# A two-layer kernel on one core: the state update ahead of the gate product, new windows for the planner, keys scaled on ScalarE, and a masked block made one slot earlier

## The chip, the core and the metric

The kernel runs on one core of a Trainium2 chip. A core has five engines with queues of their own: TensorE (PE, matmuls into PSUM), VectorE (DVE), ScalarE (ACT), GpSimd (POOL, which works on SBUF only here) and SyncE (SP, which issues the DMAs). An engine works through its own queue in order, and waits on semaphores for the others. The metric is the device time of one execution in microseconds (us); lower is better.

## The reference, cut to what matters

Two transformer-like layers over 2 x 1024 tokens of width 256. The first layer adds to the residual a gated delta-rule attention with 32 value heads (16 key heads, 128 wide) and a routed low-rank FFN; the second adds a gated linear attention and an FFN with 2:4 sparsity. The change is in the delta-rule attention only:

```
qkvz = x @ W_qkvz                      # q, k, v, z per head
q, k, v = silu(causal_conv(q, k, v))   # depthwise, 4 taps
beta = sigmoid(b); g = -exp(A_log) * softplus(a + dt_bias)
q, k = l2norm(q) / sqrt(128), l2norm(k)
for each token t:                      # per head, S is 128 x 128
    S     = S * exp(g[t])
    delta = (v[t] - k[t] @ S) * beta[t]
    S     = S + outer(k[t], delta)
    o[t]  = q[t] @ S
y = rmsnorm(o * silu(z)) * norm_w @ W_out
```

## The kernel before, in words

**Tiling.** The recurrence is done in chunks of 64 tokens of both batch rows at once: the two rows fill the lower and the upper 64 partitions. A head group is 4 value heads with 2 key heads; there are 8 groups. A unit is 512 columns (4 chunks) of one group, a pair is two chunks of a unit, so there are 64 pairs, 8 to a group. Inside a chunk the tokens' mutual dependence is a triangular matrix per head, which is inverted by blocks: blocks of 8 on VectorE (`pair_lanes`), then joined to 16, 32 and 64 by small matmuls on TensorE (`pair_inverse`).

**The chain of a chunk** (`chunk_state`). TensorE multiplies the state S with keys and queries (pks and pqs, L729). VectorE subtracts pks from the values (vtok, L732) while ScalarE scales pqs (qs, L737). TensorE applies the inverse (pf, L742), GpSimd decays S (L745), ScalarE evacuates pf (f, L750), and TensorE forms the state's increment pS (L757) and the output's inner part po (L761). Then VectorE adds po to qs (L765), multiplies with the gate z (L767), and adds pS to S (L774). The next chunk's pks needs that S.

**Around the chain.** `chunk_tokens` transposes keys and values of a chunk to token order: keys go through PSUM (pk, L689), a ScalarE copy to SBUF (kt, L692) and a GpSimd product with a weight per head and token (ktok, L697); values through pv (L701) and ScalarE (vtok, L706). `chunk_norm` squares and sums on ScalarE (gsq, L784) and makes the norm on GpSimd (L789 to L796). `chunk_output` transposes on TensorE (yT, L806), evacuates on ScalarE (yTs, L809), multiplies with W_out (out, L813) and adds to the residual on VectorE (res, L816). `conv_block` projects (pj, L152), evacuates twice on ScalarE (raw L356, conv L358) and applies three taps on VectorE (L364); the SiLU (L373) is done by ScalarE at the next block. `pair_scores` makes decays and scores: a scan on VectorE (L510), an exponential on ScalarE (L512, with a table load), products on GpSimd (L514) and VectorE (np, L520), and DMAs by SP that lay the scores out again (nat L524, natd L530, n L534). `pair_lanes` ends with E (L586) on VectorE and two DMAs through DRAM (ed L588, U L590). `pair_inverse` begins with a masked copy of the scores on GpSimd (natm, L629) and a transpose of U on VectorE (L635), then px and pyt (L607) twice, with a second masked copy between.

**The order is planned.** Each engine's order of instructions is the order in which the program emits them. A slot p emits work for several pairs at once: projections and scores of pair p, the inverse of pair p-1, the states of pair p-2, the outputs of pair p-3. Each of these is a generator with a window (lo, hi) in the slot, and `in_windows` always advances the one whose next step is due first, where step n of a chain of m steps is due at lo + (hi - lo) * (n + 0.5) / m. So a window decides where in every engine's queue an instruction stands. Odd slots also hold a unit's norms (`unit_squares`, `unit_sums`, `unit_norms`).

Of the kernel before, what the change touches and what calls it, by code (L numbers as in the profile page):

```python
# [9 lines left out]
F32 = mybir.dt.float32  # L10
AF = mybir.ActivationFunctionType
ALU = mybir.AluOpType
AX = mybir.AxisListType

P = 128
# [10 lines left out]
HPG = 4  # L26
KPG = 2
# [6 lines left out]
B = 32  # L34
# [21 lines left out]
def bcast(ap, axis, n):  # L56
    a = ap.unsqueeze(axis)
    shape = list(a.shape)
    shape[axis] = n
    return a.to_broadcast(shape)  # L60
# [218 lines left out]
PH = PC * HPG  # L279
# [269 lines left out]
def pair_lanes(k, pools, pr):  # L549


    nc, n = k.nc, pr.n8
    X = k.X8[pr.index % 2]
    new = lambda tag, *shape: pools.work.tile([P, *shape], F32, tag=tag, name=f"{tag}{pr.name}", bufs=1)
    flat = lambda a: a.rearrange("p r c -> p (r c)")
    op = nc.vector.tensor_tensor

    def at(a, r, c, *dims):

        return bass.AP(a.tensor, flat(a)[:, r * W + c : r * W + c + 1].offset, [list(flat(a).ap[0])] + [[i * W + j, m] for i, j, m in dims])  # L560

    nc.vector.tensor_copy(at(X, 0, 1, (2, 2, 4)), at(n, 0, 1, (2, 2, 4)))

    two, row, col = (4, 4, 2), (1, 0, 2), (0, 1, 2)
    still = (0, 0, 2)
    t = new("t8", W, W)
    t4 = at(t, 0, 0, (1, 0, 2), (0, 1, 2))
    op(t4, at(n, 0, 2, two, row), at(X, 2, 3, two, still), ALU.mult)
    nc.vector.tensor_copy(at(X, 0, 2, two, row), at(n, 0, 2, two, row))
    yield  # L570
    op(at(X, 0, 3, two, row), at(n, 0, 3, two, row), t4, ALU.add)
    op(t4, at(X, 1, 2, two, col), at(X, 0, 1, two, still), ALU.mult)
    yield
    op(at(X, 0, 2, two, col), at(X, 0, 2, two, col), t4, ALU.add)

    t64 = new("t64", 4, 4, 4)
    T = new("T8", 4, 4)
    four = lambda i, j: (i, j, 4)
    op(t64, at(n, 0, 4, four(1, 0), four(0, 0), four(0, 1)), at(X, 4, 4, four(0, 0), four(0, 1), four(1, 0)), ALU.mult)
    yield  # L580
    nc.vector.tensor_reduce(T, t64, AX.X, ALU.add)
    op(t64, at(X, 0, 0, four(1, 0), four(0, 0), four(0, 1)), bcast(T.rearrange("p k c -> p c k"), 1, 4), ALU.mult)
    yield
    nc.vector.tensor_reduce(at(X, 0, 4, four(1, 0), four(0, 1)), t64, AX.X, ALU.add)
    E = pools.work.tile([P, W, B // W, W], F32, tag="E", name=f"E{pr.name}", bufs=1)
    op(E, bcast(X, 2, B // W), bcast(bcast(k.place, 1, W), 3, W), ALU.mult)  # L586
    ed = k.dram.tile([P, W, B], F32, tag="ed", name=f"ed{pr.name}", bufs=2)
    nc.sync.dma_start(ed, E.rearrange("p r q c -> p r (q c)"))  # L588
    pr.U = pools.work.tile([P, PH, B], F32, tag="U", name=f"U{pr.name}")
    nc.sync.dma_start(pr.U, bass.AP(ed.tensor, ed.offset, [[B, P], [P * B, PH], [1, B]]))  # L590
    yield


def pair_decays(k, pools, pr):
# [19 lines left out]
def pair_inverse(k, pools, pr):  # L614

    nc, wk = k.nc, pools.work
    flat = lambda a: a.rearrange("p a c -> p (a c)")
    new = lambda tag, s, n=B, **kw: wk.tile([P, PH, n], F32, tag=tag, name=f"{tag}{s}_{pr.name}", **kw)
    nat = pr.nat.rearrange("p x h c -> p (x h) c")

    def masked(s):

        out = new("natm", s)
        nc.gpsimd.tensor_tensor(out, nat, bcast(k.lowT[:, s - 3, :], 1, PH), ALU.mult)  # L629
        return out  # L630

    U = pr.U
    join = masked(3)
    L = new("L", 3)
    nc.vector.transpose(flat(L), flat(U))  # L635
    yield
    for s in (3, 4):
        px = part(k, f"px{s}_{pr.name}", B)
        blocks32(k, px, join, L)
        if s < 4:  # L640
            join = masked(s + 1)
        yield
        xs = new("xs", s)
        nc.scalar.copy(xs, px)
        yield
        pyt = part(k, f"pyt{s}_{pr.name}", B)
        blocks32(k, pyt, xs, U)
        yield
        nc.vector.tensor_tensor(U, U, pyt, ALU.add)  # L649
        L = new("L", s + 1)  # L650
        nc.vector.transpose(flat(L), flat(U))
        if s < 4:
            yield


    pr.invT = k.invT[pr.index % len(k.invT)]
    invT = pr.invT.rearrange("p x h c -> p (x h) c")
    full = pr.np[:, 0].rearrange("p x h c -> p (x h) c")
    for n, r in enumerate(QUARTERS):
        (nc.gpsimd.tensor_copy, nc.scalar.copy)[n % 2](invT[r, :, r], U[r])  # L660
    yield
    px = part(k, f"px5_{pr.name}", B)
    for i in range(PH):
        for q in (0, 2):
            lo, hi = QUARTERS[q], QUARTERS[q + 1]
            nc.tensor.matmul(px[hi, i, :], full[lo, i, B:CT], L[lo, i, :], start=True, stop=True)
    yield
    xs = new("xs", 5)
    for q, copy in ((1, nc.scalar.copy), (3, nc.vector.tensor_copy)):
        copy(xs[QUARTERS[q]], px[QUARTERS[q]])  # L670
    yield
    pyt = part(k, f"pyt5_{pr.name}", B)
    for i in range(PH):
        for q in (0, 2):
            lo, hi = QUARTERS[q], QUARTERS[q + 1]
            nc.tensor.matmul(pyt[lo, i, :], xs[hi, i, :], U[hi, i, :], start=True, stop=True)
    yield
    for q, copy in ((0, nc.scalar.copy), (2, nc.vector.tensor_copy)):
        copy(invT[QUARTERS[q], :, QUARTERS[q + 1]], pyt[QUARTERS[q]])
    yield  # L680


def chunk_tokens(k, pools, x):

    nc, wk, h, c = k.nc, pools.work, x.h, x.c
    if not x.last:
        pk = four(k, f"pk{x.name}")
        for m in range(KPG):
            nc.tensor.transpose(pk[:, m, :], of_chunk(h.kq[m][:, 0], c), k.ident)  # L689
        yield  # L690
        kt = wk.tile([P, KPG, P], F32, tag="kt", name=f"kt{x.name}", bufs=1)
        nc.scalar.copy(kt, pk[:, 0:KPG, :])  # L692
        yield
        x.k = wk.tile([P, HPG, P], F32, tag="ktok", name=f"ktok{x.name}")
        pair = lambda a: a.rearrange("p (m i) c -> p m i c", m=KPG)
        wend = h.wend[:, c, :].rearrange("p (m i) -> p m i", m=KPG)
        nc.gpsimd.tensor_tensor(pair(x.k), bcast(kt, 2, 2), bcast(wend, 3, P), ALU.mult)  # L697
        yield
    pv = four(k, f"pv{x.name}")
    for i in range(HPG):  # L700
        nc.tensor.transpose(pv[:, i, :], of_chunk(h.v[i], c), k.ident)  # L701
    yield
    x.v = wk.tile([P, HPG, P], F32, tag="vtok", name=f"vtok{x.name}")
    for m in range(KPG):
        two = slice(2 * m, 2 * m + 2)
        nc.scalar.activation(x.v[:, two, :], pv[:, two, :], AF.Copy, scale=h.norm[:, c, m : m + 1])  # L706
        yield


def chunk_state(k, pools, x, scored=None):  # L710
# [3 lines left out]
    nc, wk, h, c = k.nc, pools.work, x.h, x.c  # L714
# [7 lines left out]
    if not x.first:  # L722
        pks, pqs = four(k, f"pks{x.name}"), four(k, f"pqs{x.name}")
        for s, out in ((0, pks), (1, pqs)):
            for m in range(KPG):
                two = slice(2 * m, 2 * m + 2)
# [8 lines left out]
        qs = wk.tile([P, HPG, P], F32, tag="qs", name=f"qs{x.name}")  # L735
# [13 lines left out]
    f = wk.tile([P, HPG, P], F32, tag="f", name=f"f{x.name}")  # L749
# [8 lines left out]
    po = four(k, f"po{x.name}")  # L758
# [1 line left out]
        for b, rows in halves:  # L760
            nc.tensor.matmul(po[rows, i, :], x.pair.np[rows, 1, x.at, i, :], f[rows, i, :], start=True, stop=True)  # L761
    yield
    no = po
    if not x.first:
        nc.vector.tensor_tensor(qs, qs, po, ALU.add)  # L765
        no = qs
    nc.vector.tensor_tensor(x.z, no, x.z, ALU.mult)  # L767
    yield
    if not x.last:
        for b in range(NB):  # L770
            if x.first:
                nc.scalar.copy(k.S[:, b], pS[b])
            else:
                nc.vector.tensor_tensor(k.S[:, b], k.S[:, b], pS[b], ALU.add)  # L774
    yield


# [79 lines left out]
def delta_layer(k, I):  # L857
    nc, tc = k.nc, k.tc
    with ExitStack() as ctx:
        pool = lambda name, bufs: ctx.enter_context(tc.tile_pool(name=name, bufs=bufs))  # L860
        pools = Pools()
# [32 lines left out]
        for p in range(NPAIR):  # L894
            pr = Pair()
            u, n = divmod(p, UCHUNK // PC)
            pr.index, pr.h, pr.name, pr.chunks = p, k.units[u], f"{k.units[u].name}_{n}", []
            for i in range(PC):
                x = Chunk()
# [6 lines left out]
        pair = lambda p: k.pairs[p] if 0 <= p < NPAIR else None  # L906
# [3 lines left out]
        with tc.manual_schedule(engines=ordered):  # L910
            for p in range(-2, NPAIR + 3):
# [24 lines left out]
                if pair(p - 2):  # L936
                    one, two = pair(p - 2).chunks
                    add("tokens1", 0.0, 0.4, chunk_tokens(k, pools, two))
                    add("state0", 0.0, 0.5, chunk_state(k, pools, one, pair(p)))
                    add("state1", 0.5, 1.0, chunk_state(k, pools, two), "state0", "tokens1")  # L940
                    add("norm0", 0.5, 0.95, chunk_norm(k, pools, one), "state0")
                if pair(p - 3):
                    one, two = pair(p - 3).chunks
                    add("output0", 0.0, 0.25, chunk_output(k, pools, one))
                    add("norm1", 0.0, 0.5, chunk_norm(k, pools, two))
                    add("output1", 0.55, 0.85, chunk_output(k, pools, two), "norm1")
                in_windows(k, *work)
                if pair(p) and pair(p + 2):
                    pair_decays(k, pools, pair(p + 2))
# [539 lines left out]
```

## Time and profile before

| | us |
|---|---|
| median of three runs (2954.29 to 2967.72) | 2966.99 |
| the profiled execution's own time | 2959.04 |
| its span | 2957.3 |
| until the delta layer is in steady work (FFN, gates) | about 300 |
| delta layer, 69 slots | about 2350 |
| second layer | about 307 |

In the delta layer's 2350 us (300 to 2650) PE is busy for 2119.1, VectorE 1723.5, ScalarE 1516.9, GpSimd 1441.5; the mean granted clock of TensorE is 0.97. A busy row is an average over the stretch: what sets the time is read from the waits of the engine that leads, and from the order of the instructions within one slot. In the timeline a row gives start and duration in us, engine, source line, operation, output and inputs with their shapes, the count of merged instructions, and in brackets the idle time before it with what ended it.

### The profile page before, as it was taken

How to read it: one execution, taken by the hardware profiler on the slowest of the kernel's cores; microseconds unless marked ns; L12 is line 12 of the kernel's file. 1: busy time of each engine (PE TensorE's matmuls, PEld its weight loads, DVE VectorE, ACT ScalarE, POOL GpSimd, SP SyncE). 2: the span in 40 equal slices, each digit the busy share in tenths (PEclk: the TensorE clock that was granted, in tenths of full speed). 3: DMA queues.
4: the chain of work that ended last, by engine and by line, in shares of the span. 5: the costliest groups of instructions: out<-in, count | busy, mean ns of one | idle time of the engine just before them, and what ended most of it. 6: DMA issues, size and time to landing. Idle time of an engine off the chain costs nothing.

```text
span 2957.3 us, 87624 instructions
## 1 busy us (share of the span) xinstructions
PE 2644.5 (89%) x36502; PEld 1703.3 (58%) x36502; DVE 2035.0 (69%) x3845; ACT 1723.9 (58%) x4121; POOL 1500.3 (51%) x2690
## 2 busy tenths in 40 slices
PE   6997599989989998999899989998999899889997
PEld 2444356656666666666666666666566666654465
DVE  7652577677876777777778777777787777645544
ACT  4432566666666666666666666666666676544321
POOL 2220366656665666666656665666666656630000
PEclk9998799999999999999999999999999999989999
DMA  2001111111111111111111111111111111110000
GB/s 76 4 1 57 28 31 37 31 37 38 35 35 39 35 35 35 42 28 42 28 45 28 42 34 36 28 42 35 36 32 36 28 32 26 23 56 3 1 15 15
DMA packets 265965, 95.21 MB, mean 32 GB/s; under 512 B 220513, under 2 KB 244193, under 8 KB 265569
## 3 DMA queue, kind: packets, MB, share of 16 engines
q1 hardware_dynamic: 261872, 86.67, 13.0%
q8 instruction: 287, 4.70, 0.7%
q10 hardware_dynamic: 3696, 2.95, 0.3%
q14 instruction: 110, 0.89, 0.1%
HBM read 53.63 MB, written 27.53 MB: 27 GB/s over the span
## 4 chain that ended last, share of the span: by engine, by line
PE 54%; DVE 15%; ACT 13%; POOL 10%; issue 4%; SPq 3%; DMA 2%; DVEq 0%; ACTq 0%; POOLq 0%
DVE conv L364 6%; PE pj L152 5%; PE pks L729 5%; PE z L152 5%; PE out L813 5%; PE pqs L729 4%; POOL rn L445 3%; PE pf L742 2%; PE yT L806 2%; PE y L1107 2%; PE pg L152 2%; PE base L152 2%; PE pd L1339 2%; ACT L512 2%; DVE z L767 2%
## 5 line engine op out<-in xcount | busy, mean ns | idle before, releaser
L364 DVE SCALAR_TENSOR_TENSOR conv<-raw,convw,conv 128x512 f32<-128x512 f32 x768 | 719.1, 936 | 177.1 <-ACT conv L358 153.8
L152 PE MATMUL pj<-xnT,w 128*128 128x512 f32 x1024 | 501.7, 614 | 8.6 <-DMA w<-in_W_qkvz 8.6
L729 PE MATMUL pks<-S,kq 128*64 128x256 f32 x960 | 176.5, 414 | 130.4 <-DVE S L774 90.3
L152 PEld LDWEIGHTS pj<-xnT,w 128*128 128x128 f32 x1024 | 181.3, 192 | 173.2 <-issue 168.2
L745 POOL TENSOR_TENSOR S<-S,eEnd 128x512 f32<-128x512 f32 x224 | 263.3, 1195 | 25.7 <-PE pqs L729 11.7
L813 PE MATMUL out<-wo,yTs 128*128 128x256 f32 x1024 | 252.3, 390 | 3.1 <-ACT yTs L809 3.1
L152 PE MATMUL z<-wz,xnT 128*128 128x512 f32 x512 | 248.0, 607 | 0.0
L361 POOL COPY tails<-raw 128x6 f32<-128x6 f32 x192 | 47.0, 245 | 362.3 <-ACT raw L356 361.4
L813 PEld LDWEIGHTS out<-wo,yTs 128*128 128x128 f32 x1024 | 190.7, 192 | 55.6 <-issue 28.6
L660 POOL COPY invT<-U 32x256 f32<-32x256 f32 x128 | 49.7, 388 | 317.5 <-DVE U L649 313.8
L729 PEld LDWEIGHTS pks<-S,kq 128*64 128x64 f32 x960 | 80.8, 142 | 221.4 <-issue 110.1
L356 ACT COPY raw<-pj 128x512 f32<-128x512 f32 x256 | 146.4, 572 | 103.4 <-PE pj L152 65.4
L737 ACT ACTIVATE qs<-pqs,neG 128x128 f32<-128x128 f32 x480 | 136.0, 365 | 119.0 <-PE pqs L729 119.0
L784 ACT ACTIVATE gsq<-z 128x128 f32<-128x128 f32 x512 | 159.0, 311 | 61.7 <-DVE z L767 52.5
L358 ACT ACTIVATE conv<-pj,convw 128x512 f32<-128x512 f32 x256 | 176.8, 691 | 0.0
L697 POOL TENSOR_TENSOR ktok<-kt,wend 128x512 f32<-128x512 f32 x120 | 138.6, 1155 | 70.4 <-ACT kt L692 69.8
L729 PE MATMUL pqs<-S,kq 128*64 128x256 f32 x960 | 173.7, 415 | 0.0
L732 DVE SCALAR_TENSOR_TENSOR vtok<-pks,neG,vtok 128x128 f32<-128x128 f32 x480 | 134.1, 342 | 45.5 <-PE pks L729 45.5
L373 ACT ACTIVATE kq<-conv 128x512 f32<-128x512 f32 x128 | 80.6, 630 | 141.8 <-DVE conv L364 141.1
L742 PEld LDWEIGHTS pf<-vtok,invT 128*128 128x128 f32 x1024 | 131.9, 193 | 46.1 <-issue 17.3
L607 PE MATMUL px<-L,natm 32*32 32x32 f32 x8192 | 99.0, 194 | 54.0 <-DVE L L635 24.2
L774 DVE TENSOR_TENSOR S<-S,pS 128x512 f32<-128x512 f32 x224 | 143.5, 682 | 0.8
(323 smaller groups left out, 6080.4 us busy)
## 6 DMA issues: line engine op xcount, KB each, us to landing
lb<-grows SPq DMA_DIRECT2D x128, 128.0 KB
natd<-np SPq DMA_DIRECT2D x128, 128.0 KB
w<-in_W_qkvz SPq DMA_DIRECT2D x16, 512.0 KB
nat<-np SPq DMA_DIRECT2D x256, 32.0 KB
n<-natd SPq DMA_DIRECT2D x512, 4.0 KB
ed<-E SPq DMA_DIRECT2D x64, 128.0 KB
U<-ed SPq DMA_DIRECT2D x64, 128.0 KB
wz<-in_W_qkvz SPq DMA_DIRECT2D x16, 256.0 KB
```

Of the source, the lines that this page charges most:

```text
L152: k.nc.tensor.matmul(ps, lhsT_of(kt), rhs_of(kt), start=(kt == 0), stop=(kt == KT - 1))
L356: nc.scalar.copy(chunks(raw[:, :, KSIZE - 1 :]), pv)
L358: nc.scalar.activation(chunks(y), pv, AF.Copy, scale=tap(KSIZE - 1))
L364: nc.vector.scalar_tensor_tensor(y, shifted, tap(j), y, ALU.mult, ALU.add)
L697: nc.gpsimd.tensor_tensor(pair(x.k), bcast(kt, 2, 2), bcast(wend, 3, P), ALU.mult)
L729: nc.tensor.matmul(out[rows, two, :], q, k.S[:, b, two, :], start=True, stop=True)
L737: nc.scalar.activation(qs[:, i, :], pqs[:, i, :], AF.Copy, scale=at(k.neG, i))
L742: nc.tensor.matmul(pf[:, i, :], invT[:, i, :], x.v[:, i, :], start=True, stop=True)
L745: nc.gpsimd.tensor_tensor(k.S[:, b], k.S[:, b], bcast(k.eEnd[:, b, t, h.h0 : h.h0 + HPG], 2, P), ALU.mult)
L774: nc.vector.tensor_tensor(k.S[:, b], k.S[:, b], pS[b], ALU.add)
L784: nc.scalar.activation(sq, x.z[:, i, :], AF.Square, accum_out=x.sumsq[:, i : i + 1])
L813: nc.tensor.matmul(po[:, 0:D], yT[:, i, :], wo[:, i, :], start=(i == 0), stop=(i == HPG - 1))
```

## The change

Five edits, all in the delta layer:

1. In `chunk_state` the two additions to S stand ahead of qs and z, as a step of their own.
2. Windows: the two states' chains end at 0.46 and 0.96 of the slot instead of 0.5 and 1.0; norm0 lies from 0.47 to 0.9 (0.5 to 0.95); output0 from 0.08 to 0.33 (0 to 0.25); output1 from 0.6 to 0.85 (0.55 to 0.85).
3. In `chunk_tokens` the copy kt and the GpSimd product are replaced by four ScalarE activations that read the transposed keys from PSUM and write ktok with the weight as their scale.
4. The masked copy becomes a function `joining`; the first one of a pair is made in the last step of `pair_lanes`, a slot earlier than the inverse that uses it.
5. The second masked copy uses the same function at its old place.

```diff
@@ pair_lanes
     nc.sync.dma_start(ed, E.rearrange("p r q c -> p r (q c)"))
+    pr.join = joining(k, pools, pr, 3)
     pr.U = pools.work.tile([P, PH, B], F32, tag="U", name=f"U{pr.name}")
...
+def joining(k, pools, pr, s):
+
+    out = pools.work.tile([P, PH, B], F32, tag="natm", name=f"natm{s}_{pr.name}")
+    nat = pr.nat.rearrange("p x h c -> p (x h) c")
+    k.nc.gpsimd.tensor_tensor(out, nat, bcast(k.lowT[:, s - 3, :], 1, PH), ALU.mult)
+    return out
@@ pair_inverse
-    U = pr.U
-    join = masked(3)
+    U, join = pr.U, pr.join
...
-            join = masked(s + 1)
+            join = joining(k, pools, pr, s + 1)
@@ chunk_tokens
-        kt = wk.tile([P, KPG, P], F32, tag="kt", name=f"kt{x.name}", bufs=1)
-        nc.scalar.copy(kt, pk[:, 0:KPG, :])
-        yield
         x.k = wk.tile([P, HPG, P], F32, tag="ktok", name=f"ktok{x.name}")
-        pair = lambda a: a.rearrange("p (m i) c -> p m i c", m=KPG)
-        wend = h.wend[:, c, :].rearrange("p (m i) -> p m i", m=KPG)
-        nc.gpsimd.tensor_tensor(pair(x.k), bcast(kt, 2, 2), bcast(wend, 3, P), ALU.mult)
-        yield
+        for i in range(HPG):
+            nc.scalar.activation(x.k[:, i, :], pk[:, i // 2, :], AF.Copy, scale=h.wend[:, c, i : i + 1])
+            if i % 2:
+                yield
@@ chunk_state
-    no = po
-    if not x.first:
-        nc.vector.tensor_tensor(qs, qs, po, ALU.add)
-        no = qs
-    nc.vector.tensor_tensor(x.z, no, x.z, ALU.mult)
-    yield
     if not x.last:
         for b in range(NB):
             if x.first:
                 nc.scalar.copy(k.S[:, b], pS[b])
             else:
                 nc.vector.tensor_tensor(k.S[:, b], k.S[:, b], pS[b], ALU.add)
+        yield
+    no = po
+    if not x.first:
+        nc.vector.tensor_tensor(qs, qs, po, ALU.add)
+        no = qs
+    nc.vector.tensor_tensor(x.z, no, x.z, ALU.mult)
     yield
@@ delta_layer
-                    add("state0", 0.0, 0.5, chunk_state(k, pools, one, pair(p)))
-                    add("state1", 0.5, 1.0, chunk_state(k, pools, two), "state0", "tokens1")
-                    add("norm0", 0.5, 0.95, chunk_norm(k, pools, one), "state0")
+                    add("state0", 0.0, 0.46, chunk_state(k, pools, one, pair(p)))
+                    add("state1", 0.5, 0.96, chunk_state(k, pools, two), "state0", "tokens1")
+                    add("norm0", 0.47, 0.9, chunk_norm(k, pools, one), "state0")
...
-                    add("output0", 0.0, 0.25, chunk_output(k, pools, one))
+                    add("output0", 0.08, 0.33, chunk_output(k, pools, one))
...
-                    add("output1", 0.55, 0.85, chunk_output(k, pools, two), "norm1")
+                    add("output1", 0.6, 0.85, chunk_output(k, pools, two), "norm1")
```

## The prediction, made before the changed kernel was run

> **What bounds the kernel now.** I read the page first: its engine row and its clock row.
>
> ```profile
> PE 2644.5 (89%) x36502; PEld 1703.3 (58%) x36502; DVE 2035.0 (69%) x3845; ACT 1723.9 (58%) x4121; POOL 1500.3 (51%) x2690
> PEclk9998799999999999999999999999999999989999
> ```
>
> PE leads and no engine is full. The linear-attention layer runs from about 0.3 to 2.65 ms, in slots of one chunk pair each. So I asked second who PE waits for, from 600 to 2400 us (columns: sum, times, longest):
>
> ```profile
> PE pks L729 <- DVE S L774: 68.2, 31, 3.1
> PE pks L729 <- ACT kq L373: 27.5, 12, 2.6
> PE yT L806 <- POOL z L796: 26.3, 25, 1.8
> PE px L607 <- POOL natm L629: 9.6, 6, 1.6
> ```
>
> All PE waits there sum to 150 us of 1800. The period of eight slots (one head group) is 290.3 us (the same wait, at 918.78 and at 1209.07), 36.3 a slot, so 3.0 us of a slot is waiting. Third, I read one even slot, 1004.9 to 1040.35, by engine. PE:
>
> ```profile
> 1020.65 1.98 PE L152 MATMUL pj<-xnT,w 128*128 128x512 f32 x4
> 1024.67 1.37 PE L729 MATMUL pks<-S,kq 128*64 128x256 f32 x7 [2.04 <-ACT kq L373]
> ```
>
> VectorE before that moment:
>
> ```profile
> 1019.37 1.31 DVE L364 SCALAR_TENSOR_TENSOR conv<-raw,convw,conv 128x512 f32<-128x512 f32 x1 [0.81 <-ACT conv L358]
> 1020.61 0.67 DVE L765 TENSOR_TENSOR qs<-qs,po 128x512 f32<-128x512 f32 x1
> 1021.31 0.69 DVE L767 TENSOR_TENSOR z<-qs,z 128x512 f32<-128x512 f32 x1
> 1021.92 0.74 DVE L364 SCALAR_TENSOR_TENSOR conv<-raw,convw,conv 128x512 f32<-128x512 f32 x1
> 1022.59 0.68 DVE L520 TENSOR_TENSOR np<-lb,kq 128x512 f32<-128x512 f32 x1
> 1023.18 0.74 DVE L364 SCALAR_TENSOR_TENSOR conv<-raw,convw,conv 128x512 f32<-128x512 f32 x1
> 1023.85 1.28 DVE L774 TENSOR_TENSOR S<-S,pS 128x512 f32<-128x512 f32 x2
> ```
>
> The first S ends near 1024.5 and pks starts at 1024.67: the wait is for S even where the row names kq. S stands behind five instructions that the next chunk's pks does not need. This happens mid-slot in six or seven slots of eight, for 2.0 to 3.1 us. The second chunk's S, at the slot's end, costs 0.4 to 0.8 at most.
>
> **S ahead of qs and z.** By the due times S of the first chunk is now due at 0.361 of the slot, z at 0.427; the order becomes conv, S, conv, np, qs, z, conv. S comes earlier by 1023.85 - 1020.61 = 3.2 us, more than the wait. Taken alone, the mid-slot wait falls to nothing. What is late next follows from the other edits.
>
> **The output's window, 0 to 0.25 becoming 0.08 to 0.33.** This is the term that costs. Before, yT is due at 0.031 and its evacuation yTs at 0.094, ahead of qs (0.107). Now pks and pqs go first, yT is due at 0.111, yTs at 0.174, and the matmul group out at 0.236 instead of 0.156. ACT's order becomes qs, two ktok, gsq, the exponential of lb (0.135), two ktok (0.167), yTs, xs, f. PE's order is pqs, pk, yT, px, pf, pv, out. ACT's rows in this slot:
>
> ```profile
> 1011.35 1.14 ACT L737 ACTIVATE qs<-pqs,neG 128x128 f32<-128x128 f32 x4 [2.15 <-PE pqs L729]
> 1012.36 0.32 ACT L784 ACTIVATE gsq<-z 128x128 f32<-128x128 f32 x1
> ...
> 1013.23 1.28 ACT L512 ACT_TABLE_LOAD   x1
> 1014.52 0.63 ACT L512 ACTIVATE lb<-lb 128x512 f32<-128x512 f32 x1
> 1015.06 0.35 ACT L644 COPY xs<-px 128x256 f32<-128x256 f32 x1
> ```
>
> From start to next start, counted from the end of pqs (1011.21): 0.14 to qs, qs 1.01, ktok pair 0.51, gsq pair 0.87, table load and exp 1.83, ktok pair 0.51, yTs 0.49 (1008.34 to 1008.83), about 0.1 to PE: 5.46 us. PE has meanwhile pk 0.31, yT 0.49, px 0.68, pf 0.89, pv 0.44 = 2.81. So **out waits 2.65 us** where nothing waited before; everything behind it on PE (pj, pyt, pS, po, px, pj, pks) moves with it. The trace has no such wait. Its ends: 0, if ACT ran ahead, which is excluded as qs itself waits for pqs; and 3.75, if no two activations overlap (qs and ktok 4 x 0.365 each, gsq 2 x 0.503, exp 1.28 + 0.63, yTs 0.58, 0.14 and 0.1). I take 2.65, since starts in the trace follow one another that way.
>
> [...]
>
> **The slot, summed** (even, us from its first pj; PE steps from this slot's starts). pj 1.72, kq 0.93, pks 0.86, pqs 0.97 end at 4.5. Out starts at 9.95; out 1.83, pj 1.81, pyt 0.68, pS 0.93, po 0.98, px 0.69, pj 1.8 bring pks to 18.7; before, it stood at 1024.67 - 1004.91 = 19.76. Is S there? ACT, after yTs at 9.85: xs, f, vtok 1.22, table and kq 1.83, then raw and conv behind pj (13.6) until 14.8; DVE conv 15.5, S 16.8. Yes, by 1.9. But qs, z and two convs, once done before pks, now follow S: z ends near 19.5, the last conv at 20.1. gsq of that z (ACT) stands ahead of the next raw and conv, ending 22.1; conv and vtok reach 23.9. pf of the second chunk, ready at 23.8, waits 0.2; L for px5 comes at 25.4, another 0.5. From px5 to the end as before, 9.06. Sum 34.55 against 35.44: **0.9 gained** in an even slot. An odd slot has 0.6 more on ACT (silu and square of the keys) before vtok, and ssr now follows pf: pf waits 0.8; gain about 0.35. This includes the POOL wait of yT (0.6 to 0.9), which disappears because yT stands behind pks.
>
> **Keys scaled by ACT.** Per chunk a copy (46.1/120 = 0.38 us of ACT) and a POOL product (1.155) go; four activations from PSUM come. The same form is the qs row (PSUM, 128x128, per-row scale): 0.25 to 0.365 each, taken as 136.0/480 = 0.28. ACT +0.75 per chunk, +90 us in all, already counted above where it lies in front of yTs (1.02 of the 2.65); for the other chunk ACT has room ahead of out (yTs near 26, out after 27). POOL loses 139 us of cover that nobody waited for; DVE, whose conv stretches from 0.71 to 1.6 us, may gain: 0 to 20 us, taken as 0.
>
> **First masked block with the lanes.** One POOL instruction, 0.73 us, moves from the slot's start to the previous slot's end, behind z. Its input landed half a slot earlier. Behind it stand small norm steps and the tails copy, which POOL's idle time covers; uncovered it would cost 0.7. It ends the px wait of 1.6 us once a group.
>
> **S ahead of the lanes' last step.** S of the second chunk now precedes E, so E's two DMAs leave 1.3 us later. U landed 4.0 us after E where L waited for it (1224.62 to 1228.64). L then starts about 3.4 us into the slot, vtok at 5.0 to 6.1, pf is ready at 6.0: 0.1 late, inside out's wait. With S gone early, pks at the slot's start waits for nothing. The shorter chain windows do nothing else to the order.
>
> **Sum.** A group has three regular even slots, two regular odd ones, and three around its start and end that I count at zero: 3 x 0.9 + 2 x 0.35 + 1.6 = 5.0 us; eight groups 40; in the drain four chunks save qs and z, 5. Profiled execution 2959.0 - 45 = 2914; the median of the runs, 2967, stands 8 above that execution: **2922**.
>
> **The clock.** After the mid-slot waits PE often runs at half clock: granted 0.61 and 0.54 from 1316 to 1320, after a wait of 2.03. A mean of 0.98 to 0.99 is 30 to 45 us over the layer. [...]
>
> **Rivals.**
> - More than that: out's wait doesn't trip the clock, or POOL's relief speeds DVE. For it: out is preceded by dense work. Against: equal length. 2922 - 45 = **2877**. Chance 0.17.
> - A trade one for one: out's wait equals the wait removed, and pf, px5 take the rest. **2967**, within 0.5%, which is what a measurement here can tell from no change. Chance 0.13.
> - Slower: ACT ahead of yTs. If its chain takes 6.55 rather than 5.46, each of the eight slots loses 1.1 more: 8 x 8 x 1.1 = 70 against 45 gained, **2992**. It decides from 0.7 us per slot, a chain of 6.2. For it: the single durations in the page; against: the starts in the timeline. Chance 0.20.
> - The change as summed, 2890 to 2950: chance 0.50.
>
> Eight of ten: 2865 to 2990. Faster by over 0.5%: 0.67; within: 0.13; slower: 0.20.
>
> **What would show it.** Right: pks <- S nearly gone from PE's waits, out <- yTs new at 2 to 3 us in most slots, yT <- z gone, px <- natm gone, ACT near 1815 us, POOL near 1360. Wrong: no wait at out (then ACT does run ahead, and the gain is over 100 us), out waiting over 3.3 us, or L waiting for U past 6 us of the slot.

## The result, and the profile after

| | before | after |
|---|---|---|
| median, us (four runs each) | 2963.3 | 3044.2 |
| lowest to highest | 2954.3 to 2967.7 | 3028.0 to 3054.9 |
| ratio to before, 95% interval | 1 | 1.027 [1.022, 1.033] |
| profiled execution / span | 2959.0 / 2957.3 | 3054.9 / 3053.1 |
| PE busy / not busy within the span | 2644.5 / 312.8 | 2707.1 / 346.0 |

The change costs 81 us. Of the 95.8 us between the two spans, only 33.2 are waiting: 62.6 are TensorE being busy longer with the same 36502 instructions. The page after, engine row and clock row:

```profile
PE 2707.1 (89%) x36502; PEld 1721.4 (56%) x36502; DVE 2012.4 (66%) x3845; ACT 1798.9 (59%) x4481; POOL 1337.1 (44%) x2570
PEclk9998899999999999999999999999999999999999
```

The clock row is cut to tenths and hides it; the mean granted clock from 600 to 2400 us fell from 0.99 to 0.96, over the whole span from 0.971 to 0.955. In both traces the granted clock is 1.00 or 0.50. Time at half clock rose from 175 us to 278 in the whole span (from 51 to 150 between 600 and 2400). In the kernel after, the matmuls of a pj follow one another at 0.85 us at half clock and at 0.43 at full, those of out at 0.43 and 0.22. If half of the time at half clock is lost, an estimate from these steps, the clock accounts for at most 51 of the 62.6 us. What PE waits for from 600 to 2400 us (sum, times, longest):

```profile
PE out L810 <- ACT yTs L806: 100.6, 44, 2.9
PE pf L739 <- DVE vtok L729: 25.6, 32, 1.7
PE px L666 <- DVE X L562: 12.9, 14, 1.1
```

The old waits (pks for S, yT for z, px for natm) are gone. One wait stands in their place, out for yTs, about as long and as frequent as the old one of pks. PE around it, in the even slot from 1028.45:

```profile
1035.49 0.60 PE L698 MATMUL pv<-ident,v 128*128 128x128 f32 x4
1038.99 2.67 PE L810 MATMUL out<-wo,yTs 128*128 128x256 f32 x8 [2.89 <-ACT yTs L806]
1041.45 2.94 PE L152 MATMUL pj<-xnT,w 128*128 128x512 f32 x4
```

Out and pj normally take 1.99 and 1.88 us. Here they take 5.61 together instead of 3.87, 1.7 us more; the granted clock from 1040.16 to 1043.58 is 0.50. Between 600 and 2400 us out has 41 waits of more than 0.3 us; behind 32 of them the matmul groups of the next 8 us take at least 0.5 us more than usual (a group's lower quartile in the same kernel), 66 us in all. ScalarE in the same slot:

```profile
1031.31 0.31 ACT L781 ACTIVATE gsq<-z 128x128 f32<-128x128 f32 x1 [2.00 <-DVE z L771]
...
1032.57 0.57 ACT L356 COPY raw<-pj 128x512 f32<-128x512 f32 x1
1033.04 0.69 ACT L358 ACTIVATE conv<-pj,convw 128x512 f32<-128x512 f32 x1
1033.62 1.14 ACT L734 ACTIVATE qs<-pqs,neG 128x128 f32<-128x128 f32 x4
...
1036.02 1.28 ACT L512 ACT_TABLE_LOAD   x1
1037.32 0.63 ACT L512 ACTIVATE lb<-lb 128x512 f32<-128x512 f32 x1
1037.85 0.61 ACT L693 ACTIVATE ktok<-pk,wend 128x128 f32<-128x128 f32 x2
1038.35 0.58 ACT L806 COPY yTs<-yT 128x512 f32<-128x512 f32 x1
```

From the end of pqs (1033.01) to out (1038.99) are 5.98 us, not the 5.46 of the sum. The difference stands at the top: the first squares gsq of the second chunk's z wait 2.00 us for z, which now comes behind S, E and two convs. raw and conv follow them in ScalarE's queue, so qs starts 0.61 late; in the next slot it is 1.06 (pqs ends 1070.23, qs starts 1071.29). The sum had let ScalarE wait for pqs. Over the stretch:

```profile
ACT gsq L781 <- DVE z L771: 203.8, 83, 3.3
```

### The profile page after: what moved, and what is told of

Read it like the earlier page. It is cut to its first block, busy times and chain, and to the rows that moved or that the text cites. A ratio compares the mean times of both kernels' runs of the same rounds, so it can differ in the third digit from the quotient of the medians.

```text
span 3053.1 us, 88002 instructions
## 1 busy us (share of the span) xinstructions
PE 2707.1 (89%) x36502; PEld 1721.4 (56%) x36502; DVE 2012.4 (66%) x3845; ACT 1798.9 (59%) x4481; POOL 1337.1 (44%) x2570
## 4 chain that ended last, share of the span: by engine, by line
ACT 32%; PE 31%; DVE 27%; issue 4%; DMA 3%; POOL 2%; SPq 2%; ACTq 0%; DVEq 0%; POOLq 0%
DVE conv L364 9%; PE out L810 6%; PE pj L152 6%; ACT gsq L781 4%; DVE S L765 4%; ACT conv L358 4%; ACT raw L356 3%; ACT ktok L693 3%; ACT qs L734 3%; ACT L512 2%; DVE z L771 2%; DVE qs L769 2%; ACT sq L420 2%; PE y L1104 2%; ACT yTs L806 2%
## 5 line engine op out<-in xcount | busy, mean ns | idle before, releaser
L364 DVE SCALAR_TENSOR_TENSOR conv<-raw,convw,conv 128x512 f32<-128x512 f32 x768 | 671.8, 875 | 196.1 <-ACT conv L358 168.4
L810 PE MATMUL out<-wo,yTs 128*128 128x256 f32 x1024 | 305.1, 450 | 135.6 <-ACT yTs L806 135.3
L813 DVE TENSOR_TENSOR res<-res,out 128x256 f32<-128x256 f32 x128 | 53.9, 421 | 240.0 <-PE out L810 238.1
L739 PE MATMUL pf<-vtok,invT 128*128 128x128 f32 x1024 | 153.1, 293 | 35.3 <-DVE vtok L729 33.6
L786 POOL TENSOR_TENSOR ms<-sumsq,q 128x4 f32<-128x4 f32 x128 | 44.3, 346 | 271.6 <-ACT gsq L781 271.4
L693 ACT ACTIVATE ktok<-pk,wend 128x128 f32<-128x128 f32 x480 | 151.9, 376 | 1.6
L445 POOL TENSOR_TENSOR rms<-ms,mhalf 128x4 f32<-128x4 f32 x128 | 141.1, 1103 | 1.7
L754 PE MATMUL pS<-f,ktok 64*64 64x128 f32 x3840 | 132.5, 275 | 9.4 <-ACT f L747 9.4
L793 POOL TENSOR_TENSOR z<-z,rms 128x512 f32<-128x512 f32 x128 | 137.1, 1071 | 5.9
L408 ACT ACTIVATE z<-z 128x512 f32<-128x512 f32 x128 | 77.7, 607 | 102.4 <-PE z L152 102.4
```

What stands on the lines that cost most here:

```text
L364: nc.vector.scalar_tensor_tensor(y, shifted, tap(j), y, ALU.mult, ALU.add)
L445: nc.gpsimd.tensor_tensor(out, x, k.mhalf[:, 0 : x.shape[1]], ALU.pow)
L693: nc.scalar.activation(x.k[:, i, :], pk[:, i // 2, :], AF.Copy, scale=h.wend[:, c, i : i + 1])
L739: nc.tensor.matmul(pf[:, i, :], invT[:, i, :], x.v[:, i, :], start=True, stop=True)
L793: nc.gpsimd.tensor_tensor(x.z, x.z, bcast(rms, 2, P), ALU.mult)
L810: nc.tensor.matmul(po[:, 0:D], yT[:, i, :], wo[:, i, :], start=(i == 0), stop=(i == HPG - 1))
```

## The experiments

Eighteen kernels ran. Each ratio is against runs of the kernel before on the same chip (medians 2956 to 2963 us). "Kernel after" is the changed kernel. Waits are sums from 600 to 2400 us. The kernel before differs by up to 7 us between groups of experiments, so smaller differences between two experiments of different groups mean nothing.

### The output's window: a_out0_back, b_out0_only, e_out0_late

```diff
 a_out0_back (kernel after)
-                    add("output0", 0.08, 0.33, chunk_output(k, pools, one))
+                    add("output0", 0.0, 0.25, chunk_output(k, pools, one))
 b_out0_only (kernel before)
-                    add("output0", 0.0, 0.25, chunk_output(k, pools, one))
+                    add("output0", 0.08, 0.33, chunk_output(k, pools, one))
 e_out0_late (kernel after)
-                    add("output0", 0.08, 0.33, chunk_output(k, pools, one))
+                    add("output0", 0.08, 0.4, chunk_output(k, pools, one))
```

> The changed kernel with one edit undone: output0's window is 0 to 0.25 again, so that yTs stands before qs in ACT's queue. Theory A (yTs behind the exponential makes out wait, and the wait halves the clock behind it): out's wait for yTs falls from 106 us (600 to 2400) to under 10, the mean granted clock rises above 0.97, and the time is 2870 to 2930. Theory B (the four key activations overload ACT): another wait takes its place, the time stays above 3000. Theory C (S ahead of z makes z late, so gsq and with it ACT are late in every slot): the time stays above 2963.

> The kernel before with one edit of the change alone: output0's window 0.08 to 0.33. Theory A: out waits for yTs about 2 us in most slots (a shorter ACT chain than in the changed kernel, kt instead of four activations), pks still waits for S, and the time is 3060 to 3160. Theories B and C: no slower than 2980, since neither the keys nor S are touched.

> The changed kernel with output0's window ending at 0.4 instead of 0.33: out is then due behind pj and pyt, so that two PE steps of 2.5 us lie between pv and out. Theory A (out's place ahead of ready work makes PE idle, and the idling halves the clock): out's wait falls under 20 us (600 to 2400), the clock returns to 0.97 or more, the time is 2910 to 2945. If the late start of ACT in the slot (gsq waiting for z) is the cause, another step waits instead and the time stays above 2980.

Measured: a 2924.8, ratio 0.988 [0.987, 0.990]; b 2984.1, 1.009 [1.007, 1.010], outside what was expected; e 2948.8, 0.997 [0.996, 0.999], a little above it. Undoing the window in the changed kernel gains 119 us, 60 of them busy PE (2647.0). Alone, the same window costs 25: out waits in 37 cases, 59 us in all, and seldom over 2.2. With out behind pj and pyt (e) its wait is gone altogether. So the loss needs the window, but the window is dear only in company of something else in the change.

### The other parts alone and undone: c_S_only, d_keys_back, g_keys_only, h_out0_keys_back

```diff
 c_S_only: kernel before, the additions to S moved ahead of qs and z
 g_keys_only: kernel before, with the keys on ScalarE
 d_keys_back: kernel after, with the keys' copy and product again
-        for i in range(HPG):
-            nc.scalar.activation(x.k[:, i, :], pk[:, i // 2, :], AF.Copy, scale=h.wend[:, c, i : i + 1])
...
+        nc.scalar.copy(kt, pk[:, 0:KPG, :])
...
+        nc.gpsimd.tensor_tensor(pair(x.k), bcast(kt, 2, 2), bcast(wend, 3, P), ALU.mult)
 h_out0_keys_back: d_keys_back and a_out0_back together
```

> The kernel before with one edit of the change alone: the two additions to S ahead of qs and z, windows as before. Theory A: pks' mid-slot wait for S (92 us of 600 to 2400 by S and kq together) nearly goes, the clock rises, and the time is 2840 to 2900. Theory C: slower than 2963, with ACT's gsq waiting for z about 200 us more than before. Theory B says nothing here beyond a gain.

> The changed kernel with one edit undone: keys scaled by the ScalarE copy and the GpSimd product again. Theory A: out's wait shortens by about 0.7 us a slot and stays at 1.3 to 2.2, the clock stays low, the time is 2985 to 3020. Theory B: the loss goes, at most 2965.

> The kernel before with one edit of the change alone: keys scaled by four ScalarE activations from PSUM. Theory A: ACT's chain to conv becomes 0.5 to 0.8 us longer, and with it the mid-slot wait for S; 2975 to 3010. Rival (less GpSimd work makes VectorE faster): at most 2955.

> The changed kernel with two edits undone: output0's window is 0 to 0.25 and keys are scaled by the ScalarE copy and the GpSimd product. If the key activations cost something even where out does not wait for ACT: 2890 to 2918, faster than the run with the window alone undone (2925). If their relief of GpSimd is worth more: 2930 or more.

Measured: c 2961.8, 1.001 [1.000, 1.003]; d 2975.2, 1.005 [1.004, 1.007]; g 2954.9, 1.000 [0.998, 1.002]; h 2899.1, 0.980 [0.978, 0.982]. c missed. g missed the 2975 to 3010 that it had from the first theory; it stands at the edge of the rival's 2955, but is no faster than the kernel before. d came out better than the first theory had it. S alone is worth nothing. In c, pks no longer waits for S, but ScalarE's wait for z has grown from 34 us before to 183, and PE waits for what comes late behind it:

```profile
PE ssr L429 <- ACT sq L420: 30.5, 24, 1.5
PE yT L806 <- POOL z L796: 20.3, 25, 1.8
PE out L813 <- ACT yTs L809: 16.5, 16, 1.8
PE pf L742 <- DVE vtok L732: 15.7, 18, 1.1
```

The keys cost nothing alone and 69 us in the changed kernel, where they stand ahead of yTs (out's waits of 2.2 us or more: 29 in the changed kernel, 7 in d). With output0's window undone they still cost about 25 us (a against h).

### Is it the wait, or the clock behind it: f_filler, i_filler2

```diff
 kernel after, chunk_output
     po = ps_tile(k, f"out{x.name}")
+    if x.at == 0:
+        for _ in range(4):        # f_filler; range(2) in i_filler2
+            nc.tensor.matmul(po, k.ident, k.xnT[:, 0, 0:512], start=True, stop=True)
```

> The changed kernel plus work: ahead of out of every first chunk four matmuls of the identity with xnT, 128x512 each (1.7 us at full clock, the shape of pj), into the bank that out then overwrites; the output does not change. They fill out's wait. Theory A with the clock as its larger half: the steps behind the wait run at full clock, PE's busy time rises by less than the 110 us of filler (64 x 1.72), and the time falls to 2975 to 3020 although work was added. If the clock does not depend on the wait, the time is 3044 or more.

> The changed kernel with two instead of four extra matmuls (ident x xnT, 128x512, into the output's PSUM tile, which out then overwrites) ahead of out for the first chunk of a pair. The run with four took 3.43 us of filler per slot for a wait of 2.9 at most, so it lengthened the slot by itself; two should take 1.72 us and leave about 1.2 us of waiting. The output is the same. If the half clock behind the long wait is what makes PE 63 us busier, the filler covers 1.72 us of the wait without adding to it, the clock stays up and the kernel is 25 to 60 us faster than the changed one: 2985 to 3020, granted clock 0.97 or more. If the loss is only the wait itself, the filler changes nothing: 3035 to 3055. If the slots without a wait pay for the filler, 3055 or more.

Measured: f 3052.7, 1.032 [1.030, 1.035], a miss: each fp32 matmul of 128x512 ran as two records (x4 for two of them in the row of i below), so the filler took 3.43 us per slot, longer than any wait. i 2993.8, 1.011 [1.009, 1.012], as expected if the clock costs. The page of i and one of its slots:

```profile
PE 2735.0 (91%) x36758; PEld 1716.5 (57%) x36758; DVE 2014.5 (67%) x3845; ACT 1799.6 (60%) x4481; POOL 1335.8 (45%) x2570
```

```profile
1020.99 1.88 PE L811 MATMUL out<-xnT,ident 128*128 128x512 f32 x4
1024.02 1.99 PE L813 MATMUL out<-wo,yTs 128*128 128x256 f32 x8 [1.15 <-ACT yTs L806]
1025.85 1.88 PE L152 MATMUL pj<-xnT,w 128*128 128x512 f32 x4
```

PE executes 256 instructions more, about 110 us of them (64 slots at some 1.72, the step from one such group to the next), and yet the kernel is 50 us faster than the changed one. Without the filler PE is then busy some 2625 us against 2707: by this estimate the half clock costs some 80 us in the changed kernel. The clock itself agrees: the mean granted clock of i is 0.982, against 0.955, and between 600 and 2400 us only 3 us are at half clock, against 150. Out and pj behind the rest of the wait are at full speed.

### What makes the wait long: j_norm1_late, m_S_back, r_norm1_S_back, k_norm1_late_h

```diff
 j_norm1_late (kernel after), k_norm1_late_h (h_out0_keys_back)
-                    add("norm1", 0.0, 0.5, chunk_norm(k, pools, two))
+                    add("norm1", 0.16, 0.5, chunk_norm(k, pools, two))
 m_S_back: kernel after, S behind qs and z again
 r_norm1_S_back: j_norm1_late and m_S_back together
```

In ScalarE's queue the later norm1 puts both pairs of squares of the second chunk's z behind yTs.

> The changed kernel with one window changed: norm1 from 0.16 to 0.5 of the slot instead of 0 to 0.5, so that in ScalarE's queue the squares gsq of the second chunk's z stand behind qs, ktok and yTs instead of ahead of them. If ScalarE is late for out because it first waits for z, which S ahead of z makes later, and then squares it (0.9 us and 0.6 to 1.1 us of waiting per slot), out's wait falls from 2 to 2.9 us to about 1, the clock stays up, and the kernel takes 2930 to 2990. If yTs is late for qs, the exponential and ktok alone, out still waits over 1.5 us and it takes 3020 or more.

> The same norm1 window in the fastest version so far (changed kernel with output0's window and the keys as before, 2899). There ScalarE still waits 228 us for z in steady work, but out hardly waits. If that wait reaches PE through vtok and f (pf<-vtok 23 us, pS<-f 17 us), 2880 to 2895. If it is hidden, 2895 to 2905. If the later norm makes output1 late, above 2905.

> The changed kernel with S behind qs and z again; everything else of the change stays (windows, keys on ScalarE, masked block with the lanes), and gsq keeps its place ahead of yTs. If it is the later z, and with it the first pair of gsq that ScalarE waits for at the slot's start, that makes out's wait long, gsq<-z falls from 204 us to under 80, out's wait to under 70 us, the granted clock rises to 0.97, and the time is 2930 to 2985, although pks waits for S again by some 60 us. If the gsq work ahead of yTs is enough without the waiting for z, out still waits about 100 us, pks<-S is added, and it takes 3050 to 3110.

> The changed kernel with norm1 from 0.16 and S behind qs and z again, so that output0 stays at 0.08 to 0.33 but ScalarE neither squares z nor waits for it ahead of yTs. If the squares and the later z are the whole cost of output0's window, this is as fast as the kernel with that window as before, 2880 to 2900. If the output's later place costs by itself (qs, exponential and ktok are still ahead of yTs, 1.0 us of wait per slot as in j_norm1_late), 2905 to 2940.

Measured: j 2923.3, 0.987 [0.985, 0.989], just under its range; k 2910.4, 0.981 [0.979, 0.983], whose runs (2897 to 2913) take in h, so that it decides nothing; m 2992.9, 1.012 [1.009, 1.014], just above its range; r 2955.4, 0.999 [0.998, 1.000], a miss. One number in j takes back the whole loss and more, 121 us. PE in j:

```profile
1002.93 0.60 PE L698 MATMUL pv<-ident,v 128*128 128x128 f32 x4
1005.24 1.99 PE L810 MATMUL out<-wo,yTs 128*128 128x256 f32 x8 [1.71 <-ACT yTs L806]
1007.07 1.88 PE L152 MATMUL pj<-xnT,w 128*128 128x512 f32 x4
```

Out still waits, but never longer than 1.71 us, and PE is busy 2643.3 us, as in the kernel before. So the squares ahead of yTs, and z's lateness that they wait for, lengthen out's wait to 2.0 to 2.9 us, and behind waits of that length the half clock comes (150 us of it between 600 and 2400 in the changed kernel, 17 in j). m takes away z's lateness alone: gsq's wait is no longer among ScalarE's seven largest, out's wait 71 us, pks waits for S again (29 us), 51 us gained. With S behind z, taking the squares away as well gains another 38 (r against m).

r shows that j isn't only a shorter chain. With the squares out of the way S ahead of z gains 32 us (j against r); with them in the way it costs 51 (the changed kernel against m). And output0's window costs something even there: r is 69 us above the kernel with the window as before (p, below), with 40 us of out's waits and 23 of pf's new, 23 us of pks' waits fewer, and PE busy 26 us longer; norm1 differs as well. How the rest divides stays open.

### Where the gain is: l_h_S_back, n_natm_only, o_windows_only, q_states_only, p_windows_natm_keys

```diff
 o_windows_only (kernel before); q_states_only: the first two lines alone
-                    add("state0", 0.0, 0.5, chunk_state(k, pools, one, pair(p)))
-                    add("state1", 0.5, 1.0, chunk_state(k, pools, two), "state0", "tokens1")
-                    add("norm0", 0.5, 0.95, chunk_norm(k, pools, one), "state0")
...
-                    add("output1", 0.55, 0.85, chunk_output(k, pools, two), "norm1")
+                    add("state0", 0.0, 0.46, chunk_state(k, pools, one, pair(p)))
+                    add("state1", 0.5, 0.96, chunk_state(k, pools, two), "state0", "tokens1")
+                    add("norm0", 0.47, 0.9, chunk_norm(k, pools, one), "state0")
...
+                    add("output1", 0.6, 0.85, chunk_output(k, pools, two), "norm1")
 n_natm_only: kernel before, the masked block with the lanes
 l_h_S_back: o and n together;  p_windows_natm_keys: l and the keys on ScalarE
```

> The fastest version so far with S behind qs and z again (what is left of the change: the masked block with the lanes, the shorter windows of the states and of norm0 and output1). If S ahead of z is what gains there, the wait of pks for S (68 us before) is back, and it takes 2945 to 2970. If the shorter windows and the masked block gain, 2890 to 2910, with S's order worth nothing, as it was alone.

> The kernel before with the first masked block made with the lanes, nothing else. The prediction gave this edit 1.6 us per group, 13 us: 2945 to 2960. If it is worth nothing, within 2958 to 2970.

> The kernel before with the windows of state0, state1, norm0 and output1 of the change, and nothing else. With the masked block these gave 75 us in the run without S, keys and output0's window (2887). If the windows are the whole of that, 2885 to 2905; if they need the masked block beside them, 2930 to 2965. The prediction had these windows change nothing.

> The kernel before with the windows of state0 and state1 of the change (0 to 0.46 and 0.5 to 0.96) and nothing else. In the run with all four windows (2881) pf and pS stand one place earlier in TensorE's queue (pS ahead of px instead of behind it) and the waits of pks fall from 100 to 62 us, those of yT for z from 26 to 3. If the states' windows give the pks part, 2900 to 2925, and output1 and norm0 the rest; if they give all, 2880 to 2890; if it is output1's later place, 2945 or more.

> The kernel of 2887 with the keys on ScalarE as in the changed kernel (so the changed kernel without S ahead of z and with output0's window as before). With S ahead the keys on ScalarE cost 25 us (2925 against 2899); alone they cost nothing (2955 against 2963). If ScalarE's spare time takes them when z comes early, 2880 to 2892, else 2900 to 2920.

Measured: l 2887.3, 0.975 [0.973, 0.976], and o 2880.9, **0.974 [0.972, 0.976]**, both just under a range of theirs; n 2967.6, 1.004 [1.003, 1.005], in the range named for "worth nothing" but 11 us behind its own kernel before; q 2959.2, 1.001 [0.999, 1.002], the third of its cases; p 2886.6, 0.976 [0.974, 0.978]. Four windows alone give the best kernel of the study, 163 us below the changed one. Masked block and keys add nothing to them. S ahead of z, added to l and p, costs 12 (h) and 38 us (a). The states' windows alone give nothing either: the gain comes with norm0 and output1 beside them (these two weren't run without the states'). The waits of q, then of o:

```profile
PE pks L729 <- DVE S L774: 59.3, 44, 2.2
PE yT L806 <- POOL z L796: 36.7, 25, 1.9
```

```profile
PE pks L729 <- DVE S L774: 61.7, 38, 2.3
...
PE yT L806 <- POOL z L796: 2.9, 8, 0.4
```

Over the whole span the waits of yT for z fall from 48.6 to 7.6, about as much as PE's idle time between q and o (287.5 to 250.1); its busy time falls by another 40 (2666.4 to 2626.8). The clock isn't the reason, it is 0.977 in both; most of the 40 us stands in ssr and pks, and why stays open. In n the masked copy on GpSimd keeps z late: yT waits 41.1 us for z, against 26.3 before, and of the 9.6 of px for natm, which are gone, 6.8 come back as waits of px for another GpSimd step (rstch).

## Why the prediction was wrong, by its own steps

The forecast was 45 us less, the profiled execution came 96 more. Against the forecast that is 63 us of busy time and 78 of idle time.

- **The sum has no term for a change of the clock. This is the step that failed first.** No run shows that the clock costs the same before and after; the time at half clock rose from 51 to 150 us between 600 and 2400. The row that the prediction read (a half clock behind a wait of 2.03 us) was right, and the new wait showed the same: no wait of out is longer than 2.9 us, and behind 32 of the 41 the matmuls run slow. The waiting also stayed the same, as the "equal length" set against the first rival had it: from 600 to 2400 us 101 us in 49 waits of pks before, 100 us in 41 of out after. But equal length was not equal cost. Counted in the same way in both, the slow matmuls behind the old waits cost 29 us, those behind the new ones 66. The difference, 37 us in 1800, is 48 over the layer's 2350, the greater part of the 63; the time at half clock gives at most 51. What differs is how much of a wait lies in one beat of 3.41 us, the spacing at which the granted clock changed in every trace (last section): 15 of the 37 old waits over 1.75 us and 27 of the 35 new ones have 1.95 us or more in one beat, and half clock follows each of these 42. (The size that the prediction gave the old cost is a little off too: 0.01 to 0.02 of 2350 us are 24 to 47, not 30 to 45.) Filler and j give 60 to 90 us for the half clock in the changed kernel as a whole.
- **"Out waits 2.65 us": right in kind and in size.** Of 41 waits, 26 are over 2.6. But the chain ahead of it began too early. The sum starts at the end of pqs; ScalarE came 0.6 to 1.1 later because z came later. The text moved S ahead of qs and z and followed z for the first chunk (gsq "ending 22.1"), but for the second chunk it asked only whether pks would wait. The first pair of gsq at the slot's start was left out.
- **"Taken alone, the mid-slot wait falls to nothing": the wait did, the time didn't** (c, 1.001). The wait moved to ScalarE, and from there to ssr, out and pf. S's part of the forecast is thus lost in the changed kernel, and m shows it turned into a cost of 51 us.
- **The slot, 34.55 predicted, 37.2 measured** (the even slot), the odd one 39.8. f_filler has the same even slot at 35.7 at full clock, with a filler 0.54 longer than the wait: about 35.2 without the clock. So some 2.0 of the 2.65 that the slot took more are clock by this estimate, 1.7 by out and pj alone; 0.5 is the longer chain to out (5.98 against 5.46). (The sum's last terms, 25.4 and 9.06, make 34.46; that 0.1 changes nothing.)
- **"The shorter chain windows do nothing else to the order": wrong by 75 us, to the good side** (o; what they are worth beside the rest of the change wasn't measured). The pieces of output1 and norm0 were counted only as yT's POOL wait, inside an odd slot's gain of 0.35.
- **Keys: ScalarE +75 us, predicted +90; a term inside the 2.65, as said.** Undone they give 69 back. Without S ahead of z they are free (g, p), beside it they cost 25 even where out doesn't wait (a against h); the sum had no view of what one more microsecond in that chain would do to the clock.
- **The masked block, 1.6 us gained per group: wrong**, 11 us lost (n). What happened fits "uncovered it would cost 0.7": z, for which yT waits 15 us more, is on the same queue.
- **"Table load and exp 1.83": right.** In the even slot of the changed kernel the load starts at 1036.02, the exponential 1.30 after it (1037.32), and the next ktok at 1037.85: 1.83 in all.
- **The rival "ACT ahead of yTs"** named the place and the point from which it decides, a chain of 6.2 us for the loss of 0.7 per slot, and gave it 0.20. The measured chain is 5.98 in one slot and near 6.4 in the next (0.45 more of lateness). The place was right; the price of a microsecond there was too low, since it left out the clock.
- **The signs of being right all came true**: pks for S, yT for z and px for natm gone, out for yTs new at 2 to 3 us, ScalarE at 1798.9 us, GpSimd at 1337.1. None of them was about the clock or about z, so they could not tell a gain of 45 us from a loss of 96.

## What to carry to other kernels

When a step is put earlier on a queue, follow the step that is put later to its next reader on every engine, and on to what is queued behind that reader; here the reader, a square on ScalarE, stood ahead of everything that TensorE was about to need. Judge a wait of TensorE by its length and not only by the sum: here a wait under 1.75 us nearly always cost only itself (behind 18 of 427 the matmuls were slowed), while behind about half of the longer ones (113 of 220) they were slowed. Read the granted clock over a few us behind the wait before taking two waits of one length for equal. And price a window's neighbours apart from the edit that was meant to pay: the best part of this change was the one that looked like padding.

## What the runs showed of the hardware

**Length alone does not decide.** Waits over 0.3 us from 600 to 2400 us, in the kernels before and after and the runs a, b, c, d, g, i, j, m, n, o, q and r; a case counts as slowed when the matmul groups of the next 8 us take over 0.5 us more than usual:

| wait, us | of pks: cases | slowed | of out: cases | slowed |
|---|---|---|---|---|
| under 1.75 | 224 | 5 | 203 | 13 |
| 1.75 to 2.2 | 54 | 16 | 16 | 8 |
| 2.2 to 2.6 | 23 | 16 | 36 | 21 |
| over 2.6 | 62 | 30 | 29 | 22 |

In i and j (70 waits of out, 1.71 us at most) no case is slowed. Of the longer waits, 62 of 139 are slowed at pks and 51 of 81 at out; in the two kernels of the change 15 of 37 at pks before, 27 of 35 at out after.

**The half clock goes with the idle time within one stretch of 3.41 us.** In all twenty traces the granted clock is 1.00 or 0.50, and each of its changes lies at a multiple of 3.41 us, counted from the first; I call the time between two multiples a beat. Two waits of the kernel before, and then the wait of the kernel after that was shown above, each with the beat that holds most of it and the next beat (columns: beat, us, then busy time and instructions of PE, PEld, DVE, ACT, POOL, then granted clock, DMA share, GB/s):

```profile
918.78 1.37 PE L729 MATMUL pks<-S,kq 128*64 128x256 f32 x7 [3.06 <-DVE S L774]
917.09:920.50 3.41, 1.72 (x14) 1.04 (x15) 2.15 (x4) 2.33 (x8) 0.00 (x0) 1.00 0.13 14
920.50:923.91 3.41, 3.41 (x79) 2.11 (x76) 2.74 (x7) 3.38 (x12) 0.19 (x1) 1.00 0.28 52
```

```profile
1314.99 1.37 PE L729 MATMUL pks<-S,kq 128*64 128x256 f32 x7 [2.03 <-ACT kq L373]
1313.03:1316.45 3.42, 1.46 (x12) 0.85 (x14) 2.79 (x5) 2.36 (x8) 0.19 (x1) 1.00 0.24 43
1316.45:1319.86 3.41, 3.41 (x75) 1.88 (x71) 2.08 (x6) 1.65 (x7) 0.00 (x0) 0.50 0.11 6
```

```profile
1036.75:1040.16 3.41, 1.17 (x5) 1.06 (x6) 0.70 (x1) 3.39 (x9) 2.83 (x4) 1.00 0.00 0
1040.16:1043.58 3.42, 3.42 (x7) 2.02 (x6) 1.02 (x2) 1.83 (x2) 2.19 (x8) 0.50 0.00 0
```

The wait of 3.06 us lies across an edge, with 1.7 us in this beat and the rest in the one before, and the clock stays up. The wait of 2.03 us has 1.96 in one beat, and the next beat is at half clock. All beats at full clock from 600 to 2400 us, in the twenty traces:

| PE idle within the beat, us | beats | next beat at half clock |
|---|---|---|
| under 1.0 | 9208 | 0 |
| 1.0 to 1.6 | 670 | 24 |
| 1.6 to 2.0 | 258 | 83 |
| 2.0 and more | 118 | 117 |

So half clock followed 117 of the 118 beats with 2.0 us or more of idling and none of the 9208 with less than 1.0. Between 1.0 and 2.0 us it followed 107 of 928, and what tells these from the others wasn't shown (23 of the 24 halvings below 1.6 us are at neither of the two waits). For pks and out the place plays no part that shows: at 2.0 us and more, all 49 beats whose longest wait is out's and all 50 whose longest is that of pks are followed by half clock. In the two kernels of the change, the 42 waits of pks and out with 1.95 us or more in one beat are all followed by half clock, the 27 with 1.85 or less never (3 lie between). By their lengths alone, put at random on the raster, some 22 of the 37 old waits over 1.75 us and 23 of the 35 new ones would be slowed (an estimate from the waits' lengths, with 1.9 us in one beat as the limit, between the 1.85 and the 1.95 just named); 15 and 27 were. Nor is this the accident of one execution: the mean granted clock is 0.955 to 0.964 in the four runs of the kernel after, 0.968 to 0.976 in all runs of the kernel before beside the experiments. Why the old waits lay across an edge more often than the new ones wasn't tried; a head group lasts nearly a whole number of beats in both (290.3 us are 85.05 beats, the 303.8 of the kernel after 89.0), so by these two periods a wait meets the raster much the same way group after group: the seven waits of pks of 3.02 to 3.07 us in the kernel before have 1.52 to 1.98 us in one beat.
